# Attention block with multi-query keys on one core: loads of x moved a cycle ahead, two products moved, hand-written orders of the front and the end changed, centred end rows kept in PSUM

## The chip, the cores and the metric

The kernel runs on 1 core of one Trainium2 chip. The metric is the device time of one execution in microseconds (us). Engines are called as in the profile: PE (matmul), PEld (the weight loads of PE, which overlap its matmuls), DVE (vector), ACT (scalar), POOL (GpSimd), SP (the queue that issues nearly all DMAs).

## What is computed

x has 64 sequences of 128 tokens with 512 features. Each gets a pre-normed attention with 16 heads and one shared key and value head of 64, a bias per head, a null key, a causal and a key mask, an output projection, a layer norm, and the residual.

```python
xn = layernorm(x, g_in)
q = (xn @ Wq).reshape(b, n, H, DH).transpose(0, 2, 1, 3) * scale
kv = xn @ Wkv                      # one key and one value head for all 16 query heads
sim = q @ [null_k, k]^T + [null_bias, attn_bias]
sim = where(causal or masked, neg, sim)
out = softmax(sim) @ [null_v, v]
out = layernorm(out @ Wo, g_out)
return x + out
```

## The kernel before, in words

**Tiles and stages.** A group is four sequences. Rows of x come in by `load_x(m)` (L114), one tile of 128 rows by 512 for each m; from the third group on a tile takes a quarter of each of the four sequences, in four DMAs of 64 KB. Such a tile lives in a pool of three buffers (`xp`). `norm_stats(m)` (L282, DVE, then the power -1/2 on POOL), `norm_apply(m)` (ACT, L310) and `tokens_T(m)` (DVE transposes, L331) make it normed and transposed blocks; `tokens_out(g)` (L340) sends a group to DRAM in one DMA and `tokens_in(g)` (L348) reads it back as `xT` in four. `key_values` (L1067; matmuls L358, eviction L373) makes keys and values, `values_send`, `keys_send` and `values_fetch` (L387, L393, L399) move them.

**Products by Strassen.** The query product of a group is seven products of half size instead of eight. `q_one(c, k, h)` (L973) is product k: matmuls in L597, into bank "a" or "c" or a bank of `ps_w`, then an eviction: ACT copies into kept tiles `kp`, `ku` (L608) or into `qT` (L614), DVE sums into `qT` (L617). Products 6, 7 and 4 go on adding onto bank "a" after the copy of the product before; product 3 adds onto bank "c" after DVE's sum of product 7. From cycle 2 (`LEAF`) products 2, 3 and 4 are split once more: `leaf` (L536), matmuls L553, DVE sums L556. The output projection of a pair does the same: `out_one(p, k)` (L1017), matmuls L860, with sums of its inputs on POOL (`out_sum`, L843).

**Scores and softmax.** `region(c)` (L1050) computes the scores of the next two sequences (L651) and the values of the two whose softmax is done (L770). DVE adds scores to mask and bias (L687; the sum `bias_add`, L635, is POOL's), takes maxima (L692); ACT takes exponentials (L701); POOL scales (L722); DVE transposes (`blocks_T`, L737); ACT or DVE evicts the values into `oT` (L810, L808).

**The order of the work** is written out by hand, since the schedule is manual: each engine does its instructions in the order of the program text, and waits only for data and buffers. SP takes DMAs in that order too, so a DMA that waits for its buffer holds up all DMAs behind it. There are three lists: the front (L1289 to L1446) with `q_half` (L429: four matmuls of 256 columns, each in two passes) for the first group, products of the second group, and the first scores; `cycle(c)` (L1071) for c = 1 to 29, one pair of sequences each; and the end (L1451 to L1597) for the last pairs. Even cycles end in `tokens_out` and `tokens_in` of a group (L1258, L1268).

**Padding.** `nc.tensor.addr_align(256, offset=n)` puts the next PE instruction at slot n of a block of 256 by empty instructions ahead of it.

**The end.** `y_half` (L873) gives the last six output rows tiles in SBUF (`y_end`). `stats_part` and `pair_stats` (L902, L909 to L913), `pair_pow` (L917, POOL), `pair_center` (L940: subtract the mean, times g_out, which `gain_copy` has put into PSUM) and `pair_scale` (L946: times 1/sqrt, plus the residual `res`) finish them, `store` (L960) writes them out. `load_res` (L132) loads the residual rows.

Of the kernel before, what the change touches and what calls it, by code (L numbers as in the profile page):

```python
# [17 lines left out]
def kernel(  # L18
# [59 lines left out]
    nc = tc.nc  # L78
# [855 lines left out]
    gain = [gob]  # L934

# [4 lines left out]
    def pair_center(b):  # L940
        mv, rstd = yn[b]
        nc.vector.scalar_tensor_tensor(
            ys[b], ys[b], mv[:, 0:1], gain[0], ALU.subtract, ALU.mult
        )

    def pair_scale(b):  # L946
        mv, rstd = yn.pop(b)
        nc.vector.scalar_tensor_tensor(  # L948
            ys[b], ys[b], rstd, res.pop(b), ALU.mult, ALU.add
        )  # L950
# [4 lines left out]
    def pair_residual(b):  # L955
        nc.vector.tensor_tensor(ys[b], yn.pop(b), res.pop(b), ALU.add)
# [114 lines left out]
    def cycle(c):  # L1071
# [22 lines left out]
        if m < B:  # L1094
            load_x(m)
        if fin:
            pair_pow(r)
# [83 lines left out]
        if fin:  # L1181
            pair_gain(r)
            pair_residual(r)
            store(r)
# [121 lines left out]
    q_half(0, 0)  # L1306
    weights_q(0, 1)
    norm_stats(4)
    weights_kv()
    weights_q(1, 1)  # L1310
    norm_stats(5)
    q_half(1, 0)
    weights_q(2, 1)
    norm_T(2)
    weights_q(3, 1)
    weight_sum(1)
    norm_T(3)
    norm_nmr(4)
    norm_apply(4)
    mask_neg(0)  # L1320
    q_half(2, 0)
    kv_out(0, kv_mm(0))
    kv_out(2, kv_mm(2))
    values_send(0)
    norm_nmr(5)
    null_columns()
    norm_stats(6)
    weight_sum(2)
    q_half(3, 0)
    weight_sum(4)  # L1330
    q_half(4, 0)
    norm_apply(5)
    norm_stats(7)
    norm_nmr(6)
    norm_T(4)
    q_half(5, 0)
    keys_send(0)
    null_shift(0, R8)
    bias_add(0)
    q_half(6, 0)  # L1340
    norm_nmr(7)
    norm_apply(6)
    norm_T(5)
    load_x(10)
    bias_add(1)
    q_half(4, 1)
    load_x(11)
    key_values(4)
    norm_apply(7)
    q_half(7, 0)  # L1350
    values_fetch(0)
    load_null_value()
    norm_T(6)
    norm_T(7)
    token_sum(1, 3)
    region(-1)
    exps(0, 0, 0, 4)
    q_half(5, 1)
    exps(0, 0, 4)
    exps(0, 1, 0, 2)  # L1360
    rinv(0, 0)
    q_half(6, 1)
    scores_max(1, 0)
    token_sum(1, 1)
    token_sum(1, 2)
    scale(0, 0)
    token_sum(1, 4)
    q_half(7, 1)
    q_one(0, 1, 0)
    weight_sum(3)  # L1370
    scores_max(1, 1)
    q_one(0, 2, 0)
    load_x(9)
    load_late()
    exps(0, 1, 2, 4)
    q_one(0, 6, 0)
    load_x(8)
    norm_stats(8)
    exps(1, 0, 0, 4)
    exps(0, 1, 4, 7)  # L1380
    exps(0, 1, 7)
    norm_stats(9)
    norm_stats(10)
# [4 lines left out]
    q_half(1, 1)  # L1388
    q_one(0, 5, 0)
    q_one(0, 7, 0)  # L1390
    norm_stats(11)
    norm_apply(8)
    exps(1, 0, 4)
    rinv(1, 0)
    q_half(0, 1)
    scale(1, 0)
    nc.tensor.addr_align(256, offset=31)
    q_one(0, 4, 0)
    exps(1, 1, 0, 4)
    exps(1, 1, 4)  # L1400
    blocks_T(0)
    bias_add(2)
    rinv(1, 1)
    q_one(0, 3, 0)
    scale(1, 1)
    nc.tensor.addr_align(256, offset=73)
    q_one(0, 1, 1)
    q_one(0, 2, 1)
    out_weight_sum(0)
# [3 lines left out]
    leaf_weights(2, 1)  # L1413
    tokens_T(8)
    key_values(6)
    tokens_T(9)
    leaf_weights(2, 2)
    q_one(0, 6, 1)
    nc.tensor.addr_align(256, offset=138)
    q_one(0, 5, 1)  # L1420
    q_one(0, 7, 1)
    out_weight_sum(1)
    values_send(1)
    norm_apply(10)
    norm_apply(11)
    nc.tensor.addr_align(256, offset=179)
    q_half(2, 1)
    blocks_T(1)
    bias_add(3)
    out_weight_sum(2)  # L1430
    leaf_weights(4, 1)
    q_half(3, 1)
    q_one(0, 4, 1)
    out_weight_sum(3)
    tokens_T(10)
    tokens_T(11)
    leaf_weights(3, 1)
    leaf_weights(3, 2)
    leaf_weights(3, 4)
    q_one(0, 3, 1)  # L1440
    keys_send(1)
    leaf_weights(4, 2)
    leaf_weights(4, 4)
    leaf_weights(2, 4)
    tokens_out(2)
# [8 lines left out]
    load_res(B - 2)  # L1454
# [4 lines left out]
    scores_upper(B - 2, ps_w, "ww")  # L1459
    scores_max(B - 3, 0)  # L1460
    exps(B - 4, 0, 0, 8)
    load_res(B - 4)
# [4 lines left out]
    load_res(B - 3)  # L1467
# [6 lines left out]
    rinv(B - 4, 1)  # L1474
    scores_add(B - 2, 0)
    scores_max(B - 2, 0)
    exps(B - 3, 0, 0, 8)
    scale(B - 4, 0)
# [10 lines left out]
    rinv(B - 3, 0)  # L1489
    load_res(B - 5)  # L1490
    scale(B - 3, 0)
# [7 lines left out]
    pair_pow(B - 8)  # L1499
# [4 lines left out]
    blocks_T(B - 3)  # L1504
    out_one(B - 6, 7, True)
# [12 lines left out]
    out_one(B - 4, 1)  # L1518
    pair_stats(B - 7)
    scores_max(B - 1, 1)  # L1520
# [39 lines left out]
    pair_center(B - 6)  # L1560
    out_one(B - 2, 2)
    out_sum(B - 2, 0)
# [12 lines left out]
    out_sum(B - 2, 2)  # L1575
    pair_center(B - 4)
    out_one(B - 2, 5)
# [4 lines left out]
    stats_part(B - 2, 0)  # L1582
    stats_part(B - 2, 1)
    pair_stats(B - 2)
# [7 lines left out]
    pair_stats(B - 1)  # L1592
    pair_pow(B - 1)
    store(B - 2)
# [40 lines left out]
```

## Time and profile before

| what | value |
|---|---|
| median of three runs | 1035.18 us (1034.01 to 1036.33) |
| the profiled execution, its own time | 1035.38 us |
| its span, first to last instruction | 1033.6 us |
| mean granted clock of PE | 0.997 |
| DMA | 100.90 MB, mean 98 GB/s |

In the page of the profile each engine has its busy time, its share of the span and its count of instructions. Rows of a timeline read: start in us, duration in us, engine, line, operation, output <- input, shape, count, and in brackets the idle time of that engine just before and what ended it. A group of several instructions has one row with their count; a matmul's duration reaches to its modelled end, so the starts say more than the ends. Rows of waits read: engine and line, what it waited for, total us, number of times, the longest. "issue" is a wait for nothing that the profile shows; SPq rows are the issue of DMAs.

### The profile page before, as it was taken

To read this page: it belongs to the slowest core of one execution; us is meant where nothing else is said; L and a number is where in the kernel's file an instruction comes from. 1 tells how busy PE (TensorE), PEld (TensorE's weight loads), DVE (VectorE), ACT (ScalarE), POOL (GpSimd) and SP (SyncE) were. 2 spreads that over 40 slices of the span, in tenths; PEclk is the share of its full clock that TensorE was granted. 3 is DMA by queue.
4 is the path that set the end of the run, shared out by engine and by line. 5 is a ranking of instruction groups with operands and counts; after the bars stand their busy time and mean duration, and the time that the engine had idled before them with its cause. 6 is when DMAs were issued, how large, how long until landed. Compare 5 with 4: busy or idle time off the path is not lost. (4 is left out here: it accounts for less than half of the span.)

```text
span 1033.6 us, 31778 instructions
## 1 busy us (share of the span) xinstructions
PE 1017.9 (98%) x12104; PEld 894.1 (87%) x12104; DVE 864.3 (84%) x2000; ACT 644.0 (62%) x2742; POOL 787.5 (76%) x710
## 2 busy tenths in 40 slices
PE   9999999999999999999999999999999999999996
PEld 8878888889888888888889888888888898888875
DVE  7766888888888898888888888888888988878898
ACT  2655776556775656766557765557756567755581
POOL 3699959588696877959679595886968779596774
PEclk9999999999999999999999999999999999999998
DMA  6541160522506144151521605225051431502202
GB/s 210 164 131 48 73 156 23 149 82 88 151 33 151 59 126 114 72 131 39 147 93 72 167 21 147 75 94 145 32 155 55 129 111 72 126 13 63 83 2 102
DMA packets 70263, 100.90 MB, mean 98 GB/s; under 512 B 27744, under 2 KB 31328, under 8 KB 68320
## 3 DMA queue, kind: packets, MB, share of 16 engines
q1 hardware_dynamic: 69008, 97.83, 33.3%
q8 instruction: 96, 1.57, 0.7%
q10 hardware_dynamic: 1104, 1.05, 0.3%
q14 instruction: 55, 0.45, 0.1%
HBM read 63.19 MB, written 33.55 MB: 94 GB/s over the span
## 5 line engine op out<-in xcount | busy, mean ns | idle before, releaser
L701 ACT ACTIVATE s<-s,nmax 128x65 f32<-128x65 f32 (+1 forms) x1024 | 377.0, 400 | 3.4 <-DVE nmax L692 3.4
L722 POOL TENSOR_TENSOR s<-s,rinv 128x1024 f32<-128x1024 f32 (+1 forms) x128 | 188.5, 1483 | 57.1 <-DVE rinv L718 56.6
L701 ACT ACTIVATION_READ_ACCUMULATOR s<-s,nmax 128x1 f32 x1024 | 229.2, 224 | 0.0
L635 POOL TENSOR_TENSOR s<-biasp,mneg 128x1552 f32<-128x1552 f32 x64 | 205.0, 3225 | 2.3 <-DMA x<-in_x_dram 2.0
L810 ACT ACTIVATE oT<-poX,nv 128x256 f32<-128x256 f32 x58 | 27.6, 476 | 219.8 <-PE poX L770 112.7
L556 DVE TENSOR_TENSOR qT<-pl,qT 128x128 f32<-128x128 f32 (+1 forms) x420 | 128.6, 329 | 9.5 <-PE pl L553 6.9
L687 DVE TENSOR_TENSOR s<-ps,s 128x256 f32<-128x256 f32 (+2 forms) x224 | 120.1, 604 | 15.7 <-PE ps L651 15.2
L860 PE MATMUL pyX<-wo,oT 128*128 128x256 f32 x512 | 121.5, 380 | 0.0
L692 DVE TENSOR_REDUCE nmax<-s 128x8 f32<-128x520 f32 (+1 forms) x128 | 118.8, 949 | 0.1
L860 PE MATMUL pyX<-wT,oT 128*128 128x256 f32 x488 | 115.5, 380 | 0.8 <-POOL oT L843 0.8
L737 DVE STREAM_TRANSPOSE sb<-s 128x1536 f32<-128x1536 f32 x64 | 112.9, 1764 | 0.2 <-POOL s L722 0.2
L860 PEld LDWEIGHTS pyX<-wo,oT 128*128 128x128 f32 x512 | 96.9, 190 | 14.6 <-issue 0.9
L860 PEld LDWEIGHTS pyX<-wT,oT 128*128 128x128 f32 x488 | 88.4, 190 | 10.8 <-POOL oT L843 1.2
L651 PE MATMUL ps<-kT,qT 64*64 64x128 f32 (+1 forms) x4096 | 93.6, 245 | 1.0 <-issue 1.0
L917 POOL TENSOR_TENSOR rstdo<-rstdo,nhalf 128x1 f32<-128x1 f32 x64 | 35.5, 557 | 75.6 <-PE pl L553 68.3
L651 PEld LDWEIGHTS ps<-kT,qT 64*64 64x64 f32 x4096 | 85.5, 134 | 6.0 <-issue 2.6
L289 POOL TENSOR_TENSOR rstd<-rstd,nhalf 128x1 f32<-128x1 f32 x64 | 37.3, 583 | 65.2 <-DVE rstd L288 59.2
L770 PE MATMUL pos<-sb,vr 32*64 32x128 f32 (+1 forms) x1792 | 81.8, 321 | 0.0
L770 PE MATMUL poY<-sb,vr 32*64 32x128 f32 x720 | 74.8, 347 | 0.2 <-issue 0.2
L770 PE MATMUL poX<-sb,vr 32*64 32x128 f32 x960 | 73.7, 299 | 0.0
L503 ACT COPY qT<-pa 128x256 f32<-128x256 f32 x168 | 66.7, 397 | 1.4 <-PE pa L597 1.4
L860 PE MATMUL pyw<-wo,oT 128*128 128x256 f32 x280 | 66.4, 380 | 0.3 <-POOL oT L843 0.2
(150 smaller groups left out, 2514.8 us busy)
## 6 DMA issues: line engine op xcount, KB each, us to landing
res<-in_x_dram SPq DMA_DIRECT2D x64, 256.0 KB, 3.0
out_dram<-y SPq DMA_DIRECT2D x58, 256.0 KB, 2.0
x<-in_x_dram SPq DMA_DIRECT2D x224, 64.0 KB, 2.7
xd<-xb SPq DMA_DIRECT2D x14, 1024.0 KB, 3.9
xT<-xd SPq DMA_DIRECT2D x56, 256.0 KB, 5.9
vr<-vd SPq DMA_DIRECT2D x64, 128.0 KB, 2.7
x<-in_x_dram SPq DMA_DIRECT2D x8, 256.0 KB, 4.9
vd<-vt SPq DMA_DIRECT2D x32, 64.0 KB, 2.2
```

What stands on the lines that cost most here:

```text
L289: nc.gpsimd.tensor_tensor(rstd, rstd, nhalf, ALU.pow)
L503: nc.scalar.copy(q_part(g, c, h), by_block("a"))
L556: nc.vector.tensor_tensor(o, p, o, ALU.add)
L635: nc.gpsimd.tensor_tensor(S[b], biasp, mneg[:, t].unsqueeze(1).broadcast_to([P, R8, ROW]), ALU.add,)
L651: nc.tensor.matmul(to[r][i * DH : (i + 1) * DH, f, :], qT[g, f // FH, t // GH][rows, f % FH, t % GH, NQ - 1 - i if hf else i], kT[g][rows, ...
L687: nc.vector.tensor_tensor(sv, ps, sv, ALU.add)
L692: nc.vector.tensor_reduce(nmax[b][:, hf], S[b][:, :, WITH_NULL[hf]], AX.X, ALU.max, negate=True)
L701: nc.scalar.activation(row, row, AF.Exp, bias=nmax[b][:, hf, k : k + 1], accum_out=rsum[b][:, hf, k : k + 1],)
L722: nc.gpsimd.tensor_tensor(sv, sv, rinvs.pop((b, hf)).unsqueeze(2).broadcast_to([P, R8, sv.shape[2]]), ALU.mult,)
L737: nc.vector.transpose(sb.rearrange("p j e q -> p e j q"), S[b][:, :, 1 : ROW - 1].rearrange("p e (j k) -> p e j k", k=Q),)
L770: nc.tensor.matmul(po[s][rows, half], vr[g][quad(s), j, t, :], sb[quad(s), slots, r * NF : (r + 1) * NF, :], start=start, stop=True, skip_ ...
L860: nc.tensor.matmul(prod[key], h[:, c, :], w[:, c, :], start=(start and c == 0), stop=(c == HC - 1), skip_group_check=not start,)
```

## The change

1. **Loads of x.** `load_x(m)` and `load_x(m + 1)`, which each cycle issued for its own use, go. Each cycle now issues `load_x(m + 2)` ahead of `store(r)` and `load_x(m + 3)` ahead of `tokens_out`, for the next cycle; cycle 1 issues its own two at its start as well.
2. **Two products of cycle 1** (the only pass of `cycle` with c < LEAF): product 4 goes behind `out_one(p, 2)`, product 3 goes ahead of product 1 of the other half.
3. **The front.** The list after `q_half(0, 0)` is in a new order, for all engines; the offsets of the paddings are 40, 97, 146 and 211 in place of 31, 73, 138 and 179.
4. **The end.** Some steps of its list trade places.
5. **Centred rows.** For the last six rows `pair_center` writes into a PSUM tile (two rows a tile, tag "s"), and `pair_scale` reads that and writes `ys`.

```diff
     def pair_center(b):
         mv, rstd = yn[b]
+        if b < B - 6:
+            o = ys[b]
+        else:
+            if b // 2 not in yns:
+                yns[b // 2] = ps_s.tile([P, 2, DIM], FP, tag="s", name=f"yc_{b}")
+            o = y_mid[b] = yns[b // 2][:, b % 2]
         nc.vector.scalar_tensor_tensor(
-            ys[b], ys[b], mv[:, 0:1], gain[0], ALU.subtract, ALU.mult
+            o, ys[b], mv[:, 0:1], gain[0], ALU.subtract, ALU.mult
         )
...
-            ys[b], ys[b], rstd, res.pop(b), ALU.mult, ALU.add
+            ys[b], y_mid.pop(b, ys[b]), rstd, res.pop(b), ALU.mult, ALU.add
...
-        if m < B:
+        if c == 1:
             load_x(m)
+            load_x(m + 1)
...
         q_one(c, 7, 0)
-        if m + 1 < B:
-            load_x(m + 1)
...
         if c >= LEAF:
             q_one(c, 8, 0)
-        else:
+        out_one(p, 2)
+        if c < LEAF:
             q_one(c, 4, 0)
-        out_one(p, 2)
...
             exps(b0, 1, 0, 6)
+        if c < LEAF:
+            q_one(c, 3, 0)
         q_one(c, 1, 1)
...
-        if c < LEAF:
-            q_one(c, 3, 0)
...
             pair_residual(r)
+        if m + 2 < B:
+            load_x(m + 2)
+        if fin:
             store(r)
...
             q_one(c, 4, 1)
+        if m + 3 < B:
+            load_x(m + 3)
         if first and toks:
             tokens_out(m // GB)
```

The new front, PE's steps in their order with the padding, and of the others the steps that the text below names (`...` where steps are left out):

```python
q_half(0, 0); weights_kv(); weights_q(2, 1); q_half(1, 0); norm_T(2); weights_q(3, 1); norm_T(3); load_x(11)
...
q_half(2, 0); kv_out(0, kv_mm(0)); kv_out(2, kv_mm(2)); weight_sum(1); weight_sum(2); values_send(0)
q_half(3, 0); keys_send(0); q_half(4, 1); q_half(4, 0); null_shift(0, R8); bias_add(0); bias_add(1)
q_half(5, 0); norm_T(4); norm_T(5); q_half(7, 0); key_values(4); norm_T(6); q_half(6, 0); load_x(10); norm_T(7)
region(-1); token_sum(1, 3); scores_max(1, 0); weight_sum(4)
q_half(5, 1); load_late(); rinv(0, 0); load_x(9); q_half(6, 1); q_one(0, 1, 0); q_half(7, 1); weight_sum(3)
q_one(0, 2, 0); q_one(0, 5, 0); q_one(0, 6, 0); load_x(8); values_fetch(0); q_half(1, 1); q_one(0, 7, 0)
q_half(0, 1); q_one(0, 4, 0); addr_align(256, offset=40)
q_one(0, 3, 0); key_values(6); norm_apply(10); q_one(0, 1, 1); addr_align(256, offset=97)
q_one(0, 2, 1); q_half(2, 1); blocks_T(1); out_weight_sum(0); bias_add(3); addr_align(256, offset=146)
q_one(0, 6, 1); values_send(1); keys_send(1); q_one(0, 5, 1); q_one(0, 7, 1); q_half(3, 1); addr_align(256, offset=211)
q_one(0, 4, 1); tokens_T(11); tokens_out(2); q_one(0, 3, 1); region(0)
```

The old one from the same place, PE's steps:

```python
q_half(5, 1); q_half(6, 1); q_half(7, 1); q_one(0, 1, 0); q_one(0, 2, 0); q_one(0, 6, 0); q_half(1, 1); q_one(0, 5, 0)
q_one(0, 7, 0); q_half(0, 1); addr_align(256, offset=31); q_one(0, 4, 0); q_one(0, 3, 0); addr_align(256, offset=73)
q_one(0, 1, 1); q_one(0, 2, 1); key_values(6); q_one(0, 6, 1); addr_align(256, offset=138); q_one(0, 5, 1); q_one(0, 7, 1)
addr_align(256, offset=179); q_half(2, 1); q_half(3, 1); q_one(0, 4, 1); q_one(0, 3, 1); region(0)
```

The end, the parts that matter:

```diff
-    out_one(B - 6, 2)
+    out_one(B - 6, 5)
+    out_one(B - 6, 2)
+    scores_add(B - 1, 0)
     scores_upper(B - 1, ps_s, "s")
-    out_one(B - 6, 5)
...
     pair_center(B - 5)
     out_sum(B - 2, 1)
     out_sum(B - 2, 3)
+    pair_scale(B - 5)
     pair_pow(B - 3)
-    pair_center(B - 3)
     pair_scale(B - 6)
     store(B - 6)
-    pair_scale(B - 3)
-    store(B - 3)
-    pair_scale(B - 5)
+    out_one(B - 2, 5)
     store(B - 5)
     pair_pow(B - 4)
+    pair_center(B - 3)
+    pair_scale(B - 3)
     out_sum(B - 2, 2)
     pair_center(B - 4)
-    out_one(B - 2, 5)
+    stats_part(B - 2, 0)
     pair_scale(B - 4)
```

Beside these, residual loads are issued in another order at the start of the end's list, and `pair_pow(B - 8)`, `pair_stats(B - 7)`, `scale`, `store(B - 3)` and `store(B - 2)` move by a few places.

More of the change, by code (lines that the diff above doesn't have):

```diff
@@ L1323 @@
     kv_out(2, kv_mm(2))
+    weight_sum(1)
+    norm_apply(5)
+    weight_sum(2)
     values_send(0)
-    norm_nmr(5)
+    q_half(3, 0)
+    norm_stats(6)
+    norm_nmr(6)
+    keys_send(0)
     null_columns()
-    norm_stats(6)
-    weight_sum(2)
-    q_half(3, 0)
-    weight_sum(4)
[L1331 to L1357, printed above, removed]
-    q_half(5, 1)
[L1359 to L1363, printed above, removed]
+    q_half(4, 1)
+    norm_stats(7)
+    q_half(4, 0)
+    null_shift(0, R8)
+    norm_nmr(7)
+    bias_add(0)
+    bias_add(1)
@@ L1364 @@
+    q_half(5, 0)
+    norm_apply(6)
+    norm_T(4)
+    norm_T(5)
+    q_half(7, 0)
+    norm_apply(7)
+    key_values(4)
+    norm_T(6)
+    q_half(6, 0)
+    load_x(10)
+    norm_T(7)
+    region(-1)
+    token_sum(1, 3)
+    exps(0, 0, 0, 4)
+    scores_max(1, 0)
+    weight_sum(4)
+    q_half(5, 1)
     token_sum(1, 1)
     token_sum(1, 2)
+    load_late()
+    exps(0, 0, 4)
+    rinv(0, 0)
+    exps(0, 1, 0, 2)
+    load_x(9)
+    q_half(6, 1)
+    scores_max(1, 1)
     scale(0, 0)
     token_sum(1, 4)
+    q_one(0, 1, 0)
```

109 lines of the change are left out of this document (55 added, 54 removed).

## The prediction

> **What bounds the kernel now.** I read the shares of the engines first, then the starts of the scores along PE's timeline, then the waits, at last the few windows where PE stands still.
>
> ```profile
> PE 1017.9 (98%) x12104; PEld 894.1 (87%) x12104; DVE 864.3 (84%) x2000; ACT 644.0 (62%) x2742; POOL 787.5 (76%) x710
> ```
>
> PE is the bound nearly everywhere, and the change takes no matmul away. So it can win only where PE stands, and after PE's last matmul. How much PE stands in the cycles is read from the starts of the score matmuls, one row for each cycle:
>
> ```profile
> 128.45 2.91 PE L651 MATMUL ps<-kT,qT 64*64 64x128 f32 x128
> ...
> 566.30 2.91 PE L651 MATMUL ps<-kT,qT 64*64 64x128 f32 x128
> 597.34 2.91 PE L651 MATMUL ps<-kT,qT 64*64 64x128 f32 x128
> 628.44 2.91 PE L651 MATMUL ps<-kT,qT 64*64 64x128 f32 x128
> 661.03 2.91 PE L651 MATMUL ps<-kT,qT 64*64 64x128 f32 x128
> ...
> 941.21 2.91 PE L651 MATMUL ps<-kT,qT 64*64 64x128 f32 x128
> ```
>
> An odd cycle can take 31.04 us (566.30 to 597.34), an even one 31.10 (597.34 to 628.44), yet the odd one from 628.44 takes 32.59. From the first row to the last are 13 odd and 13 even cycles in 812.76 us; at 62.14 a pair they would take 807.8. So **4.9 us** are lost there, 1.55 of them in the one cycle. Who is late:
>
> ```profile
> PEld pl L553 <- DVE qT L556: 6.4, 14, 1.0
> ```
> ```profile
> DVE st L284 <- DMA x<-in_x_dram: 8.0, 9, 2.0
> ```
> ```profile
> 630.91 4.34 SPq L348 DMA_DIRECT2D xT<-xd  x4
> 636.94 7.11 SPq L128 DMA_DIRECT2D x<-in_x_dram  x8
> ```
> ```profile
> 644.30 0.69 DVE L284 BATCH_NORM_STATS2 st<-x 128x6 f32<-128x512 f32 x1 [1.98 <-DMA x<-in_x_dram]
> ```
> ```profile
> 645.98 0.49 PE L553 MATMUL pl<-xL,wq 128*128 128x128 f32 x2 [0.59 <-DVE qT L556]
> ```
>
> Between 110 and 960 us PE's weight loads wait 14 times for the sums of the small products (6.4 us), and in the cycles between 180 and 960 us DVE waits 9 times for a tile of x (8.0 us). The rows of the bad cycle join the two: SP issues x behind the four reads of xT, eight issues take 7.11 us, the statistics of x stand 1.98 us for the tile, the sum behind them comes that late, and PE stands for the sum.
>
> **Part 1, loads a cycle ahead.** A tile then has a whole cycle of some 31 us in hand, where the first is now issued 7.4 us before its use (636.94 to 644.30), so DVE's 8.0 us of waits go. Not all of that was PE's loss: the upper bound is the 4.9 us above, a lower one the 1.55 of this cycle alone. I take **-4.4**, near the upper end, since the sums are the only wait besides steady ones in this stretch, and leave 0.5 for what may belong to others. What is late next in an undisturbed cycle is nothing on PE: 31.04 is reached now.
>
> What the moved loads pass on SP: in an odd cycle `load_x(m + 2)` stands behind the reads of the values and ahead of a store which is not ready for some time anyway; in an even cycle `load_x(m + 3)` comes ahead of the send of the tokens:
>
> ```profile
> 618.94 0.70 DVE L331 STREAM_TRANSPOSE xb<-x 128x512 f32<-128x512 f32 x1
> ```
> ```profile
> 623.70 0.33 SPq L340 DMA_DIRECT2D xd<-xb  x1
> 629.49 1.25 SPq L387 DMA_DIRECT2D vd<-vt  x2
> ```
> ```profile
> 642.63 1.89 PE L358 MATMUL pkv<-xT,wkv 128*128 128x256 f32 x8
> ```
>
> Its buffer is free once the transpose at 618.94 is done, at 619.64. Four issues at the slowest rate seen above (7.11 / 8 = 0.89 us) end at 623.2, ahead of 623.70. So the send isn't late: cost nothing, covered by the time in which SP waits for the second transpose.
>
> **Parts 2 and 3, cycle 1 and the front.** PE's standing there:
>
> ```profile
> 50.62 1.03 PE L597 MATMUL pc<-xT,wS 128*128 128x256 f32 x4
> 51.99 1.13 PE L597 MATMUL pa<-xT,wq 128*128 128x256 f32 x4 [0.35 <-ACT qT L614]
> ...
> 55.55 1.03 PE L597 MATMUL pa<-xS,wS 128*128 128x256 f32 x4
> 57.16 1.10 PE L597 MATMUL pc<-xS,wS 128*128 128x256 f32 x4 [0.58 <-DVE kT L373]
> ```
> ```profile
> 74.94 1.03 PE L597 MATMUL pa<-xS,wq 128*128 128x256 f32 x4
> 76.58 1.13 PE L597 MATMUL pa<-xS,wq 128*128 128x256 f32 x4 [0.61 <-ACT ku L608]
> 77.55 1.89 PE L860 MATMUL pyw<-wo,oT 128*128 128x256 f32 x8
> 79.28 1.03 PE L597 MATMUL pa<-xT,wq 128*128 128x256 f32 x4
> ```
>
> Eight matmuls of 256 columns take 1.73 us (77.55 to 79.28), a product of four 0.87. So the first two gaps are 51.99 - 50.62 - 0.87 = 0.50 and 57.16 - 55.55 - 0.87 = 0.74; PE's next start behind such a gap is 0.1 late again (76.58 to 77.55 is 0.97). Front: 1.4 us can be won; cycle 1: 76.58 - 74.94 - 0.87 + 0.1 = 0.87.
>
> I followed the new front by hand with the durations of the trace, each engine in its new order. Up to the first scores PE finds everything in time; tightest is `key_values(4)`, ready 0.1 us ahead. Behind them, product (0, 3, 0) comes right when DVE's sum of product 7 is done, since `weight_sum(4)`, a further 1.2 us, now stands ahead of it; and (0, 6, 1) comes some 0.3 before ACT's copy, which has `norm_apply(10)` ahead of it. Padding by offsets less matmul slots (four each) is 25 empty instructions in three places as before, one more in the first: taken as nothing, as these run ahead of PE's queue. Of 1.4 us some 0.3 come back: **-1.1**, with bounds of -1.4 and +1.4 (the same waits kept and as much again).
>
> In cycle 1 product 4 behind `out_one(p, 2)` has its copy in time. But ACT now evicts product 4 about 0.9 later, so its exponentials are later by that, while PE runs 0.9 earlier; ACT has idle 1.1 us before the copies later in the cycle, so about 0.6 of the gain is lost before product 3 of the second half. And the reads of xT for group 2 start behind four more loads:
>
> ```profile
> 68.46 2.28 SPq L348 DMA_DIRECT2D xT<-xd  x4
> ```
>
> They move from 68.46 to about 70; 4.34 us is the longest issue of such four above, and the key product that needs them would start at 79 instead of 81. That is in time, but barely. I take **-0.2** (bounds: -0.87 and +1.5).
>
> **Part 4, the list of the end.** Product 5 ahead of product 2 covers a wait for a bank, but the next stop is POOL's sum, whose chain starts at the same matmul as before:
>
> ```profile
> 988.92 1.99 PE L860 MATMUL pyw<-wo,oT 128*128 128x256 f32 x8 [0.19 <-POOL oT L843]
> ```
>
> PE starts again at 988.92 either way: **0**. Bounds: 0.5 either way, PE's standing there.
>
> **Part 5, the tail.** PE's last matmuls start at 1023.72, but DVE still has work:
>
> ```profile
> 1017.30 1.39 DVE L942 SCALAR_TENSOR_TENSOR y_end<-y_end,mvo,gain 128x512 f32<-128x512 f32 x2
> 1018.61 0.90 DVE L948 SCALAR_TENSOR_TENSOR y_end<-y_end,rstdo,res 128x512 f32<-128x512 f32 x1
> 1019.96 2.42 DVE L948 SCALAR_TENSOR_TENSOR y_end<-y_end,rstdo,res 128x512 f32<-128x512 f32 x2 [0.44 <-POOL rstdo L917]
> ...
> 1027.59 0.41 DVE L885 TENSOR_TENSOR y_end<-pyw,kyu 128x256 f32<-128x256 f32 x1
> ...
> 1029.84 0.75 DVE L948 SCALAR_TENSOR_TENSOR y_end<-y_end,rstdo,res 128x512 f32<-128x512 f32 x1
> ```
> ```profile
> 1023.72 1.89 PE L860 MATMUL pyw<-wT,oT 128*128 128x256 f32 x8
> ```
> ```profile
> L942 DVE SCALAR_TENSOR_TENSOR y_end<-y_end,mvo,gain 128x512 f32<-128x512 f32 x6 | 4.3, 737 | 0.0
> L948 DVE SCALAR_TENSOR_TENSOR y_end<-y_end,rstdo,res 128x512 f32<-128x512 f32 x6 | 5.6, 943 | 0.7 <-POOL rstdo L917 0.4
> L953 DVE TENSOR_TENSOR yn<-yn,gob 128x512 f32<-128x512 f32 x56 | 38.9, 694 | 10.3 <-ACT yn L932 10.3
> ```
>
> The six with both inputs in SBUF take 943 ns, 0.90 to 1.21 while POOL sums and 0.75 alone; the six with `gain` in PSUM hold 737 beside the same sums. With one input in PSUM the scales should hold some 0.74: 5.6 - 6 x 0.74 = 1.2 saved. The 0.44 for POOL's power goes too, as two scales now stand ahead of the one that needs it: 1.6. The trace has no such scale writing from PSUM; L953 reads and writes PSUM in 694 ns, so its bounds are 0.69 and 0.94, the gain 0.4 to 1.9. [...]
>
> Does PE then decide? Its last result is there at 1023.72 + 1.73 = 1025.5 and some latency, and DVE takes it at 1027.59, 2.1 later. A gain of 1.6 leaves DVE behind PE still. I take **-1.4**, as a scale waits some 0.1 for the step ahead of it in either form.
>
> **Sum**, against the profiled execution's own 1035.38: -4.4 - 1.1 - 0.2 + 0 - 1.4 = -7.1, which gives **1028.3 us**. That execution stands 0.2 above the median shown.
>
> **Rivals.**
> - *Front and cycle 1 give all back* (a new wait for each one removed, ACT and DVE being full there): 1035.4 - 4.4 - 1.4 = 1029.6; with their upper bounds, 1032.5. For it: two margins of 0.1 us and none above 0.5. Against: PE's gaps there are three and each has new work in it. Chance 0.23.
> - *The loads don't pay*: DVE's wait was only what showed first, and the sums are late for another cause in the same cycles (the reads of xT, say); then part 1 gives 0 to -1: 1035.4 - 0.5 - 2.7 = 1032.2. Against: nothing else is late at 644.30. Chance 0.10.
> - *No net change*: parts 1 and 5 as in the rival above, and the front loses 2: about 1035. Chance 0.08.
> - *Slower: the loads hold up the tokens.* SP is in order, so where the four loads of an even cycle issue slower, the send of 623.70 goes late.
>
> ```profile
> xd<-xb SPq DMA_DIRECT2D x14, 1024.0 KB, 3.9
> xT<-xd SPq DMA_DIRECT2D x56, 256.0 KB, 5.9
> ```
>
> The send has 630.91 - 623.70 - 3.9 = 3.3 us before the reads of xT notice, and these land by 630.91 + 4.34 + 5.9 = 641.2, 1.5 ahead of the key product. From 619.64 the loads would have to take over 4.1 + 4.8 = 8.9 us, 2.2 an issue. Beyond that 14 even cycles pay each: at 2.4 an issue 14 x 0.7 = 10 us, which gives 1028.3 + 10 = 1038. Against: 0.89 is the slowest mean seen. Chance 0.12.
>
> **Chances.** The forecast's case has 0.47, with 1026.5 to 1029.5 of its own. Faster by over 0.2% (2.1 us, about what a measurement of this kernel tells from no change): 0.47 + 0.23 + 0.08 of the second = 0.78; within 0.2%: 0.02 + 0.08 = 0.10; slower: 0.12. The range is 1025.5 to 1035.5: its low end is the sum of the best bounds (-4.9 - 1.4 - 0.9 - 0.5 - 1.9 = -9.6), the high end takes in the first three rivals.
>
> **What will show it.** Part 1: no row of DVE waiting for x in the cycles, and all odd cycles near 31.04, so 941.21 - 128.45 falls to about 808.3. Parts 2 and 3: the first scores of `region(0)`, now at 64.36, start near 63.2, with no wait of PE for ACT's copies. Part 4: the product at 988.92 still waits for POOL. Part 5: scales near 0.74, and from PE's last matmul to the end of the span 1.4 us less. The prediction is wrong if xT comes late in cycle 1 or in odd cycles (key products waiting for a DMA), or if PE meets waits for its instructions in new places.

## The result, and the profile after

The changed kernel takes **1027.64 us** (median of four runs, 1027.56 to 1027.81); the kernel before took 1034.6 beside it (1033.1 to 1036.33). The ratio is 0.9932, with a 95% interval of 0.9915 to 0.9950: faster by 0.7%. The profiled execution has 1027.59 us and a span of 1025.8 at a clock of 0.999; the span before was 1033.6.

From the page of the changed kernel, its row of engine shares:

```profile
PE 1013.1 (99%) x12104; PEld 895.4 (87%) x12104; DVE 863.5 (84%) x2000; ACT 643.9 (63%) x2742; POOL 785.7 (77%) x710
```

DVE and ACT are as busy as before. From its timeline, the scores that open the regions -1, 0 and 1, those of cycle 3, of three cycles in the middle and of cycle 29:

```profile
33.89 2.91 PE L651 MATMUL ps<-kT,qT 64*64 64x128 f32 x128
63.73 2.91 PE L651 MATMUL ps<-kT,qT 64*64 64x128 f32 x128
95.53 2.91 PE L651 MATMUL ps<-kT,qT 64*64 64x128 f32 x128
127.25 2.91 PE L651 MATMUL ps<-kT,qT 64*64 64x128 f32 x128
...
593.18 2.91 PE L651 MATMUL ps<-kT,qT 64*64 64x128 f32 x128
624.27 2.91 PE L651 MATMUL ps<-kT,qT 64*64 64x128 f32 x128
655.30 2.91 PE L651 MATMUL ps<-kT,qT 64*64 64x128 f32 x128
...
934.90 2.91 PE L651 MATMUL ps<-kT,qT 64*64 64x128 f32 x128
```

The cycle that took 32.59 takes 655.30 - 624.27 = 31.03; from cycle 3 to cycle 29 it is 934.90 - 127.25 = 807.65 us, 5.1 less. What waits for x there is gone. Rows of waits between 110 and 960 us, first PE's weight loads and then DVE (what waits, for what: total, times, longest):

```profile
PEld pa L597 <- issue: 10.4, 27, 0.4
PEld poX L770 <- issue: 4.6, 27, 0.2
PEld pa L597 <- ACT qT L503: 4.4, 15, 0.7
PEld pa L597 <- POOL rstdo L917: 4.3, 13, 0.3
PEld pl L553 <- DVE qT L1008: 0.3, 1, 0.3
```
```profile
DVE rinv L718 <- ACT s L701: 36.1, 57, 1.1
DVE y L885 <- PE pyY L860: 31.2, 27, 1.3
DVE qT L1008 <- ACT qT L503: 11.7, 39, 0.3
```

PE's 14 waits for the small sums (6.4 us) and DVE's waits for x (8.0 us) have no row any more; what is left is the steady part of each cycle.

The starts of the scores cut every kernel into stages. This table is the main tool of the study: each column is a difference of two such starts in one profiled execution, "end" runs from the scores of the last region to the end of the span.

| kernel | to first scores | front | cycle 1 | cycle 2 | 3 to 28 | cycle 29 | end |
|---|---|---|---|---|---|---|---|
| before | 33.86 | 30.50 | 32.34 | 31.75 | 812.76 | 30.06 | 62.33 |
| changed | 33.89 | 29.84 | 31.79 | 31.73 | 807.65 | 30.04 | 60.85 |
| loads alone | 33.59 | 30.53 | 32.33 | 31.77 | 807.76 | 30.05 | 62.46 |
| changed, old front | 33.61 | 30.58 | 31.80 | 31.72 | 807.67 | 30.04 | 60.59 |
| changed, old cycle 1 | 33.93 | 29.84 | 32.33 | 31.73 | 807.68 | 30.05 | 60.94 |
| changed, centred rows in SBUF | 34.01 | 29.84 | 31.79 | 31.73 | 807.76 | 30.05 | 61.71 |
| changed, old end, SBUF | 33.68 | 29.78 | 32.27 | 31.75 | 807.76 | 30.06 | 62.51 |
| changed, padding ahead of q_half | 33.49 | 29.52 | 31.80 | 31.75 | 807.76 | 30.06 | 61.52 |
| changed again | 33.55 | 29.82 | 32.27 | 31.73 | 807.76 | 30.05 | 60.80 |
| changed, padding ahead of the wait | 34.37 | 28.94 | 31.80 | 31.77 | 807.76 | 30.05 | 61.31 |
| changed, order of cycle 1 | 35.62 | 29.84 | 31.51 | 32.03 | 807.76 | 30.06 | 61.49 |
| changed, padding and reads | 33.94 | 28.94 | 31.79 | 31.73 | 807.76 | 30.06 | 61.08 |

The 7.8 us of span are 5.1 in the cycles, 0.66 in the front, 0.55 in cycle 1 and 1.48 in the end. The first column lies anywhere from 33.49 to 35.62, and the last from 60.59 to 61.52 for the eight kernels that have the changed end, so a small edit is read from its own stage and not from the whole time.

### The profile page after: what moved, and what is told of

Same layout as the page of the kernel before. It is cut to its first block, busy times and chain, and to the rows that moved or that the text cites. A ratio compares the mean times of both kernels' runs of the same rounds, so it can differ in the third digit from the quotient of the medians.

```text
span 1025.8 us, 31861 instructions
## 1 busy us (share of the span) xinstructions
PE 1013.1 (99%) x12104; PEld 895.4 (87%) x12104; DVE 863.5 (84%) x2000; ACT 643.9 (63%) x2742; POOL 785.7 (77%) x710
## 3 DMA queue, kind: packets, MB, share of 16 engines
q8 instruction: 96, 1.57, 0.7%
HBM read 63.19 MB, written 33.55 MB: 94 GB/s over the span
## 5 line engine op out<-in xcount | busy, mean ns | idle before, releaser
L701 ACT ACTIVATION_READ_ACCUMULATOR s<-s,nmax 128x1 f32 x1024 | 231.7, 226 | 0.0
L917 POOL TENSOR_TENSOR rstdo<-rstdo,nhalf 128x1 f32<-128x1 f32 x64 | 35.0, 548 | 80.4 <-PE pl L553 74.2
```

Source lines behind the costliest of these rows:

```text
L701: nc.scalar.activation(row, row, AF.Exp, bias=nmax[b][:, hf, k : k + 1], accum_out=rsum[b][:, hf, k : k + 1],)
```

## The experiments

The theory: each part of the change works in its own stage, by the waits that the forecast named. The rivals: the loads pay only together with the front, or the order of SP's queue is itself the harm; the end was won by its list and not by PSUM.

**Loads alone** (the kernel before with part 1).

```diff
-        if m < B:
-            load_x(m)
+        if c == 1:
+            load_x(m)
+            load_x(m + 1)
...
+        if m + 2 < B:
+            load_x(m + 2)
         if fin:
             store(r)
...
+        if m + 3 < B:
+            load_x(m + 3)
```

> The kernel before with part 1 alone (loads of x a cycle ahead). Theory (x came late behind the reads of xT, its lateness went through DVE's statistics and sums to PE): the stretch from the scores of cycle 3 to those of cycle 29 falls from 812.8 to about 807.6 us, all odd cycles at 31.03 to 31.04; front and end stay as before; so about 1030 us (1029.7 to 1030.5), and its runs lie within a few tenths of each other instead of 3 us. Rival (the loads pay only together with the new front or the moved products, or the sums are late for another cause in the same cycles): 1033 to 1035, with odd cycles still up to 1.5 us too long.

Measured: 1030.31 us (1029.7 to 1031.19) against 1034.58, ratio 0.9963 (0.9951 to 0.9976). Its row of the table has the whole gain of cycles 3 to 28 and nothing else. The rival is out: the loads pay by themselves, 5.0 us in the profile. Its runs spread over 1.5 us, less than the 3.7 of before beside it, but not the few tenths that were expected.

**Four places for the loads** (the changed kernel, the place of the next odd cycle's loads changing with the even cycle).

```diff
+        own = c % 2 and c > 1 and (c // 2) % 4 == 3
+        late = (c // 2) % 4 if first else 0
...
+        if late == 2 and m + 2 < B:
+            load_x(m + 2)
+        if late in (1, 2) and m + 3 < B:
+            load_x(m + 3)
```

> The changed kernel with the loads for the next odd cycle at four places in turn, by even cycle: as changed; the second tile behind the four reads of xT; both tiles behind them; both in the odd cycle itself at the old places. One kernel, read by the length of each odd cycle. Theory (what counts is whether the tile has landed when DVE comes to its statistics about 16 us into the cycle): the first three all take 31.03, since loads right behind the reads land some 3 us ahead; only the fourth is longer, by 0.1 to 1.5. Rival (to stand behind the reads is the harm itself): second and third are longer too, in this order.

Measured: 1027.83 us (one execution). Behind the reads of xT, one tile or both: 31.03 in all of these cycles (3, 5, 11, 13, 19, 21). So to stand behind the reads is no harm in itself. Loaded in the odd cycle itself: 31.03, 31.12 and 31.15 (cycles 7, 15, 23). In the second of these DVE waited, from the timeline of this run:

```profile
514.29 0.69 DVE L284 BATCH_NORM_STATS2 st<-x 128x6 f32<-128x512 f32 x1 [0.51 <-DMA x<-in_x_dram]
```

and in the kernel before, three of its ten such rows:

```profile
142.84 0.70 DVE L284 BATCH_NORM_STATS2 st<-x 128x6 f32<-128x512 f32 x1 [0.51 <-DMA x<-in_x_dram]
...
205.83 0.69 DVE L284 BATCH_NORM_STATS2 st<-x 128x6 f32<-128x512 f32 x1 [1.01 <-DMA x<-in_x_dram]
...
518.46 0.69 DVE L284 BATCH_NORM_STATS2 st<-x 128x6 f32<-128x512 f32 x1 [1.40 <-DMA x<-in_x_dram]
```

Set beside the excess of the cycle over 31.04, all ten waits of before give one rule:

| DVE's wait, us | 0.23 | 0.36 | 0.40 | 0.51 | 0.61 | 0.96 | 1.01 | 1.04 | 1.40 | 1.98 |
|---|---|---|---|---|---|---|---|---|---|---|
| the cycle's excess, us | 0 | 0 | 0 | 0.08 | 0.18 | 0.54 | 0.58 | 0.62 | 0.97 | 1.55 |

PE loses what DVE waits beyond 0.43 us, to within 0.02. The run with four places fits it: 0.51 gave 0.09, and a wait of 0.54 in cycle 23 gave 0.12; cycle 7 had no wait and lost nothing. One even cycle of that run (24) took 31.27; the next experiment comes back to it.

**The send held up** (the changed kernel, the tile ahead of the send loaded 0 to 3 times over).

```diff
+        if first and m + 3 < B:
+            for _ in range(c // 2 % 4):
+                for i in range(GB):
+                    nc.sync.dma_start(
+                        out=xs[m + 3][quad(i)],
+                        in_=x[(m + 3) // GB * GB + i, 3 * Q : 4 * Q, :],
+                    )
         if first and toks:
             tokens_out(m // GB)
```

> The changed kernel with the second tile of an even cycle loaded again 0, 1, 2 or 3 times over, in turn by cycle, ahead of the send of the tokens; each repeat waits for the one before to land and so holds SP up for some 3.5 to 4 us more. It adds 64 KB x 4 a repeat and changes no result. It measures from which lateness of the send a cycle gets longer: the forecast's rival of a slower kernel had 4.8 us of room (3.3 until the reads of xT notice, 1.5 more until the key product of the next odd cycle). Theory: one repeat is free, two cost 0 to 2 us in the next odd cycle, three cost 3 to 6 us. If the room is smaller than worked out, one repeat costs already; if it is larger, two and three are free.

Measured: 1031.48 us (one execution), but not by the curve that was expected. The send stands 4.74 us ahead of the odd cycle's scores in the changed kernel; here, by repeats (times from the starts of the scores; the fetch is the start of the first 16 KB packet of the instruction queue q8 around these scores, from the trace's DMA records):

| repeats | odd cycles | send, to the scores | fetch, to the scores | cycle, us |
|---|---|---|---|---|
| 0 | 9, 17, 25, 27 | -4.71, -4.72, -4.59, -4.74 | -0.52, -0.55, -0.35, -0.42 | 31.06, 31.04, 31.04, 31.04 |
| 1 | 3, 11, 19 | -3.82, -4.47, -4.27 | -0.13, -0.34, -0.41 | 31.04, 31.04, 31.05 |
| 2 | 5, 13, 21 | -2.36, -2.46, -2.18 | +1.77, +1.72, +1.93 | 32.32, 32.15, 32.39 |
| 3 | 7, 15, 23 | -0.29, +1.13, -0.34 | -0.36, -0.52, -0.36 | 31.04, 31.39, 31.04 |

With three repeats the send is 4.4 us late twice at no cost, and 5.9 us late once for 0.36 (PE's key product waits 0.3 there). So the room lies between 4.4 and 5.9 us; the forecast had worked out 4.8. The cost at two repeats, 1.1 to 1.35, is another thing, with PE standing inside the region. From the timelines of SP and PE in cycle 13:

```profile
436.35 0.42 SPq L340 DMA_DIRECT2D xd<-xb  x1
...
441.99 1.99 SPq L348 DMA_DIRECT2D xT<-xd  x4
```
```profile
442.83 0.32 PE L770 MATMUL pos<-sb,vr 32*64 32x128 f32 x2 [0.72 <-issue]
```

PE waits there for nothing that the profile shows. The DMA view of 440.4 to 441.6 us has a packet of instructions:

```profile
q8 instruction: 1, 0.02, 4.8%
```

Where the send goes out 2.2 to 2.5 us ahead of the scores, the fetch, elsewhere 0.1 to 0.6 ahead of them, begins only 4.1 to 4.2 us behind the send, at +1.7 to +1.9. Where the send goes out later still, the fetch has begun before it. That the fetch queues behind the 1 MB of the send is read from these times, the same in all three cycles of a kind; no run moved the fetch by itself, so it is likely and not shown.

A late fetch also goes with the even cycles that took too long. In cycles 4 and 12 of the kernel before (31.36 and 31.29 us) and in cycle 24 of the run with four places (31.27) it begins 0.80, 0.73 and 0.79 us behind the scores, and PE loses 0.26, 0.19 and 0.18 inside the region. In all other cycles from 3 to 28 of the fourteen profiles, those with two repeats apart, it begins at +0.44 or earlier, and no such cycle is longer by more than 0.04 us, but for what DVE's waits or the late send account for. In the six cycles with a late fetch PE goes on 1.4 to 1.6 us after the packet's end. The even cycles have no send, so what made the fetch late there is open. All three follow an odd cycle that loads x at the old place: there are 16 such even cycles in the profiles, and none of the 166 others has it.

**The old front** (the changed kernel; the list from `q_half(0, 0)` to `region(0)` and its offsets as before, as the change's diff shows them).

> The changed kernel with the old front: order and offsets of the kernel before from q_half(0, 0) to region(0), all else as changed. Theory (the front gave 0.66 us, from two waits less and one new standing of 0.83): the stretch from the scores of the first to those of the second region goes from 29.84 back to 30.50, so 1028.2 to 1028.4, unless cycle 1 takes part of it back. Rival (the front's order also carries part of what cycle 1 shows, since ACT and DVE enter it in another order): 1028.7 or more, with cycle 1 longer than 31.79 too.

Measured: 1028.75 us (1027.84 to 1029.95), ratio 0.9950 (0.9938 to 0.9963). The front goes back to 30.58, cycle 1 stays at 31.80: theory. The median is 0.4 above what the stage gives, within the scatter of its runs.

**The padding.** The rows that the changed kernel's front rests on, of PE and then of its sequencer:

```profile
49.79 1.03 PE L597 MATMUL pa<-xS,wq 128*128 128x256 f32 x4
51.48 0.45 PE L597 MATMUL pc<-xT,wS 128*128 128x256 f32 x1 [0.67 <-issue]
```
```profile
L1414 PEldq NOP  x30: 13/13/13, 49.1 to 51.4; - x30
```

Product 4 ends its issue at 49.79 + 0.87 = 50.66 and product 3 starts at 51.48: PE stands 0.82. The 30 empty instructions of `addr_align(256, offset=40)` take 2.3 us, and end right there. In the kernel before the same 30 ran 45.9 to 48.2, well ahead. Here they begin only at 49.1, since the sequencer, in order, has stood until 49.0 for ACT's copy which product 4 waits for, and that copy ended at 48.59 + 0.37 = 48.96:

```profile
48.59 0.37 ACT L608 COPY ku<-pa 128x256 f32<-128x256 f32 x1
```

The kernel before had the same standing in another place. Its third padding, of 25, begins when product 6 has ACT's copy (54.95 + 0.36 = 55.31) and ends where product 5 starts:

```profile
L1419 PEldq NOP  x25: 13/13/13, 55.4 to 57.1; - x25
```
```profile
55.20 0.37 DVE L617 TENSOR_TENSOR qT<-pc,ku 128x256 f32<-128x256 f32 x1
```

PE had work until 55.55 + 0.87 = 56.42, and product 5 started at 57.16. The row in the prediction puts this gap down to DVE's eviction of the keys (L373). But product 5 neither reads the keys nor writes their bank, and the last reader of its own bank, the sum of DVE above, was done at 55.57. So the 0.74 us that the forecast counted as a wait for DVE were the padding's own. This is read from the rows; no run moved that padding alone.

For the padding of the changed kernel two places were tried.

```diff
     leaf_weights(2, 1)
+    nc.tensor.addr_align(256, offset=16)
     q_half(0, 1)
     q_one(0, 4, 0)
...
-    nc.tensor.addr_align(256, offset=40)
     q_one(0, 3, 0)
```

> The changed kernel with the first padding of the front put ahead of q_half(0, 1), at offset 16 instead of 40, so that every matmul keeps its place in the block of 256 and the same 30 empty instructions stand 24 places earlier. Theory (PE stands 0.83 us ahead of product (0, 3, 0) since the 30 empty instructions, 71 ns each, stand right behind a wait of the sequencer for ACT's copy): the empty instructions are done before that wait, the standing goes, the scores of region(0) start 0.6 to 0.8 earlier, about 1026.9 us. Rival (product (0, 3, 0) in truth waits for DVE's sum of product 7, as the forecast had it): PE stands at the same place as long, 1027.6.

Measured: 1027.66 us (1027.08 to 1027.83). Neither: the front gains 0.32 of 0.83. The empty instructions (31 by the trace, not 30) now end at 48.1 and PE stands ahead of `q_half(0, 1)`:

```profile
L1407 PEldq NOP  x31: 13/13/13, 45.7 to 48.1; - x31
```
```profile
46.80 1.03 PE L597 MATMUL pa<-xS,wq 128*128 128x256 f32 x4
48.16 1.97 PE L437 MATMUL pq<-xT,wq 128*128 128x256 f32 x8 [0.34 <-issue]
```

PE has work until 46.80 + 0.87 = 47.67, so the lead at 45.7 was 1.97 us, for 2.4 of padding. In the changed kernel it was 50.66 - 49.1 = 1.56. The next place lies 16 instructions on, still ahead of the wait:

```diff
     q_half(0, 1)
+    nc.tensor.addr_align(256, offset=32)
     q_one(0, 4, 0)
```

> The changed kernel with the first padding between q_half(0, 1) and q_one(0, 4, 0), at offset 32: the same 30 empty instructions, now ahead of the sequencer's wait for ACT's copy and not right behind it, and behind the earlier wait by 16 instructions more than in the run with the padding ahead of q_half(0, 1), where PE still stood 0.58. Theory (the cost is the lead that the sequencer has over PE when it comes to the padding): PE stands nowhere from the scores of the first region to those of the second but for the steady restarts, that stretch falls from 29.84 to about 29.0, and the time by 0.6 to 0.8 against the changed kernel beside it, less what the wait for instructions in the end's list takes back (it was 0.83 in the changed kernel's profile, 0.56 to 1.5 in others). Rival (these 2.1 us of empty instructions cost 0.6 to 0.8 wherever they stand): 29.5 or more.

```profile
L1408 PEldq NOP  x31: 13/13/13, 46.6 to 49.0; - x31
```
```profile
47.68 1.03 PE L597 MATMUL pa<-xS,wq 128*128 128x256 f32 x4
48.54 1.89 PE L437 MATMUL pq<-xT,wq 128*128 128x256 f32 x8
50.27 1.03 PE L597 MATMUL pa<-xS,wq 128*128 128x256 f32 x4
51.13 1.03 PE L597 MATMUL pc<-xT,wS 128*128 128x256 f32 x4
```

The front takes 28.94: the theory. The padding ends 1.3 us ahead of product 4 (50.27), and nothing stands. The time, 1027.72 (1027.06 to 1028.75), is 0.4 below that of the changed kernel beside it, 1028.12 (1027.68 to 1028.63). The profiled execution began its first scores 0.8 later and lost 0.5 in the end, so the whole time does not settle it; the stage does.

**Old products in cycle 1** (the changed kernel; product 4 ahead of `out_one(p, 2)`, product 3 behind `leaf(c, 2, 1)` again).

> The changed kernel with the two products of cycle 1 at their old places. Theory (product 4 stood 0.78 us for ACT's copy, and half of the gain is lost again ahead of product 3 of the second half): the stretch from the scores of region(0) to the next goes from 31.79 back to about 32.3, 1028.1 to 1028.3. Rival (cycle 1 gained by the loads or the front, and not by the products): 31.8 stays, 1027.6.

Measured: 1028.34 us (1027.93 to 1028.73), cycle 1 at 32.33. Theory: 0.54 is the products' own. The sequencer stood 1.47 us for the reads of xT in this profile, but PE has no gap ahead of the key product, so the reads have no part in it.

**The changed kernel again.**

> The changed kernel once more, unaltered, on the chip of the next two runs: what they are measured against. 1027.6 as at first, if the reads of xT in cycle 1 are always just in time; up to 0.7 more in some executions if not.

Measured: 1028.12 us, and in its profiled execution cycle 1 took 32.27. So it did in the run with the old end, which shares this code. PE's sequencer on the key product's line, in this run and then in the changed kernel's first profile (shortest, median, longest wait):

```profile
L358 PEldq EVENT_SEMAPHORE  x2: 51/866/1682, 78.0 to 78.1; - x2
```
```profile
L358 PEldq EVENT_SEMAPHORE  x2: 51/51/51, 78.4 to 78.5; - x2
```

The sequencer stood 1.68 us for the reads of xT, which the two loads of cycle 1 had pushed back, and PE stood 0.74 ahead of the key product. The cycle is longer by 0.48 only, since PE, later by then, no longer waits 0.4 ahead of product 3 of the second half.

**Order of cycle 1** (the changed kernel).

```diff
         if c == 1:
             load_x(m)
-            load_x(m + 1)
...
             tokens_in(2)
+            load_x(m + 1)
...
-        if toks:
+        if toks and c >= LEAF:
             norm_apply(m + 1)
...
+        if toks and c < LEAF:
+            norm_apply(m + 1)
```

> The changed kernel with two steps of cycle 1 moved: the reads of xT go between its two loads of x (as before the change), and norm_apply(m + 1) goes behind q_one(c, 7, 1), so that ACT's copy of product 7 no longer stands behind it. Theory: the wait of 0.40 ahead of product 3 of the second half goes, cycle 1 takes about 31.4 instead of 31.79, and the key product has the reads 1.5 us earlier, so the executions in which it waited (0.74 in the profile of the run with the old end) are gone: 0.4 less than the changed kernel beside it, and a spread of a few tenths. Rival (DVE's transposes behind the moved norm come late and PE waits there instead): 31.8 or more.

Measured: 1028.24 us (1027.82 to 1030.09). The wait ahead of product 3 is gone and cycle 1 takes 31.51, but cycle 2 takes 32.03 in place of 31.73: moving `norm_apply` won 0.28 and gave 0.30 back. The 0.30 stand ahead of one small product of cycle 2, which starts 0.41 us late for a sum of DVE where it was 0.10 late: the rival in kind, one cycle later. The path from the moved norm to that sum was not traced.

**Centred rows in SBUF** (the changed kernel; `pair_center` writes `ys[b]` for all rows).

> The changed kernel with the centred rows of the end back in SBUF, in the new order of the end. Theory (a scale with both inputs in SBUF is slowed while POOL sums): in the new order about half of the six scales lie beside POOL's work, those take 0.9 to 1.2 instead of 0.75, so 0.4 to 0.7 longer than the changed kernel's 1027.6: 1028.0 to 1028.3. If all six are slowed as the forecast's term had it: 1.2 longer, 1028.8. Rival (the new order of the end won it all): no change, 1027.6, and the scales near 0.75 though they read SBUF.

Measured: 1028.87 us (1028.68 to 1029.34). The end is 0.86 longer. Its scales, from DVE's timeline, with POOL's work beside them:

```profile
1011.46 2.09 DVE L950 SCALAR_TENSOR_TENSOR y_end<-y_end,rstdo,res 128x512 f32<-128x512 f32 x2
...
1014.30 1.44 DVE L950 SCALAR_TENSOR_TENSOR y_end<-y_end,rstdo,res 128x512 f32<-128x512 f32 x1
...
1016.66 0.73 DVE L950 SCALAR_TENSOR_TENSOR y_end<-y_end,rstdo,res 128x512 f32<-128x512 f32 x1
```
```profile
1011.07 1.27 POOL L843 TENSOR_TENSOR oT<-oT 128x512 f32<-128x512 f32 x1
...
1013.93 1.27 POOL L843 TENSOR_TENSOR oT<-oT 128x512 f32<-128x512 f32 x1
```

and the six scales of the changed kernel as one group:

```profile
L955 DVE SCALAR_TENSOR_TENSOR y_end<-yc,rstdo,res 128x512 f32<-128x512 f32 x6 | 4.4, 746 | 0.3
```

It is not that all six are slower. The pair from 1011.46 takes 2.09 for 1.41 in the changed kernel, the one from 1014.30 takes 1.44 for 0.75, and the others take 0.73 to 0.75. So two of six are longer, by 0.68 and 0.69, and both are issued while a sum of POOL runs. At 1.43 and 1.44 us they are longer than the 0.9 to 1.2 of the theory. The second ends at 1015.74, and POOL's sum at 1015.20 (its spans are rough), 0.54 before. The same holds in two more kernels with the rows in SBUF: the longer scales take 0.90 and 1.75 in the kernel before, 0.92 and 1.76 with the old end, 1.43 and 1.44 here, and each ends 0.54 or 0.55 us behind the end of a sum of POOL. By these ends they wait for that sum, they are not merely slowed. With one input in PSUM nothing like it shows: in the changed kernel two scales begin beside POOL's sum of 1011.05 to 1012.31 and one beside that of 1013.31 to 1014.58, and they take 0.74 to 0.75 like the other three. Why DVE waits for POOL when both inputs are in SBUF was not shown. POOL's work is longer there too: its power (L917) takes 0.55 us as a rule, but 1.01 in the kernel before where it begins at 1018.92 beside the scale of 0.90 (1.00 beside the long scales of the other two), and that power is the one that DVE then stood 0.44 for.

**The old end, rows in SBUF** (the changed kernel with the old list of the end, and `pair_center` writing `ys[b]`).

> The changed kernel with the old list of the end and the centred rows in SBUF (parts 4 and 5 undone). Theory: the stretch from the scores of the last cycle to the end goes back from 60.85 to about 62.3 us, so 1029.1. What it is longer than the run with the centred rows in SBUF alone is the share of the new order: by the forecast about 0.4 (the wait for POOL's power), at most 1. Rival (the 1.5 us of the end came with the other parts, through PE's restarts at the start of the list): under 0.7 longer, 1028.3 or less.

Measured: 1029.42 us (1028.43 to 1029.85). The end is 62.51, as before the change, and 62.51 - 61.71 = 0.80 longer than with the rows in SBUF alone. Two rows cut the end into three parts: a group of score matmuls early in the list, and the last sum of the pair before the last. Here is first the one and then the other, each for the kernel before, the changed one, the one with rows in SBUF and this one:

```profile
978.57 1.50 PE L651 MATMUL ps<-kT,qT 64*64 64x64 f32 x58 [0.95 <-issue]
```
```profile
971.93 1.50 PE L651 MATMUL ps<-kT,qT 64*64 64x64 f32 x58 [0.40 <-issue]
```
```profile
971.95 1.50 PE L651 MATMUL ps<-kT,qT 64*64 64x64 f32 x58 [0.40 <-issue]
```
```profile
972.66 1.50 PE L651 MATMUL ps<-kT,qT 64*64 64x64 f32 x58 [0.40 <-issue]
```
```profile
1012.21 0.41 DVE L885 TENSOR_TENSOR y_end<-pyw,kyu 128x256 f32<-128x256 f32 x1
```
```profile
1005.57 0.41 DVE L885 TENSOR_TENSOR y_end<-pyw,kyu 128x256 f32<-128x256 f32 x1
```
```profile
1005.60 0.41 DVE L885 TENSOR_TENSOR y_end<-pyw,kyu 128x256 f32<-128x256 f32 x1
```
```profile
1006.40 0.41 DVE L885 TENSOR_TENSOR y_end<-pyw,kyu 128x256 f32<-128x256 f32 x1
```

| kernel | from the scores of the last region to the first row, us | on to the second row | on to the end of the span |
|---|---|---|---|
| before | 7.30 | 33.64 | 21.39 |
| changed | 6.98 | 33.64 | 20.23 |
| changed, centred rows in SBUF | 6.76 | 33.65 | 21.30 |
| changed, old end, SBUF | 7.37 | 33.74 | 21.40 |

In the tail PSUM won 1.07 of 1.16 and the order 0.09. In the middle part, where the list has product 5 ahead of product 2, nothing is won. The first part has the same matmuls in every kernel, and PE's only waits there are for nothing that the profile shows, as where a packet of instructions came late: with the new list it takes 6.76 to 7.68 us in the profiles, with the old one 7.30 to 7.41. So 0.61 of the 0.80 lie within this scatter, and the list's own share is at most 0.2. The same scatter took back what the padding's first place had won in the front (7.68 there).

**Padding and reads together** (the changed kernel; padding ahead of the wait, and the reads of xT between the two loads).

```diff
             tokens_in(2)
+            load_x(m + 1)
...
     q_half(0, 1)
+    nc.tensor.addr_align(256, offset=32)
     q_one(0, 4, 0)
```

> The changed kernel with the first padding ahead of the wait (as in the run that took the front's stretch to 28.94) and with the reads of xT of cycle 1 between its two loads of x again; norm_apply stays where the change has it, since cycle 2 gave back what cycle 1 won by it. Theory: front stretch 28.9 to 29.0, cycle 1 always 31.8 and never 32.3, so the two stretches together 60.7 to 60.8 instead of 61.6 (or 62.1 when the reads came late); the time 0.9 below the changed kernel where its reads were just in time, 1027.0 or a little above, as the start of the program and the wait for instructions in the end scatter by as much. Rival (the loads behind the reads come late for DVE's statistics in cycle 1): cycle 1 at 32 or more.

Measured: **1027.16 us** (1026.80 to 1028.95) against 1033.94, ratio 0.9937 (0.9924 to 0.9951). Front 28.94, cycle 1 31.79 in its profile. The lowest median and the lowest single run of the study, but over the whole time it can't be told from the changed kernel (0.9939, 0.9927 to 0.9952, in its second measurement).

## Why the prediction was right, point by point

- **Loads** (forecast -4.4, bounds -1.55 to -4.9): -5.1, and -5.0 alone. Mechanism right, size too small by 0.7. The mechanism of the forecast, DVE's wait for x in the odd cycles, is worth 4.52 (the sum of the table's excesses), close to the 4.4. The even cycles that had lost 0.26 and 0.19 came back too, and there the fetch of instructions was late (0.80 and 0.73 us behind the scores), which the forecast did not see. That the wait of PE follows from DVE's wait for x was argued from one cycle; the table of ten waits shows it.
- **The send is not held up** (nothing): right. 623.70 - 597.34 = 26.36 before; 619.53 - 593.18 = 26.35 after, by this row of SP:

```profile
619.53 0.34 SPq L340 DMA_DIRECT2D xd<-xb  x1
```

- **Front** (-1.1): -0.66. The step that failed is "taken as nothing, as these run ahead of PE's queue". The empty instructions cost 0.82, as a wait stands just ahead of them. The trace of the kernel before had it already: of the two gaps that the forecast read as waits for ACT and DVE, the second was padding (0.74). Of the two waits that the forecast put in their place, product (0, 3, 0) for DVE's sum and (0, 6, 1) for ACT's copy, neither is there once the padding is moved: the front is then 30.50 - 28.94 = 1.56 shorter than before, more than the bound of 1.4.
- **Cycle 1** (-0.2): -0.55 where the reads of xT were in time, -0.07 where they were not. Both parts of the working hold: ahead of product 3 of the second half 0.4 comes back (0.6 forecast), and the reads are "in time, but barely". The forecast took one value for what is two cases, and missed both. The key product that waits for a DMA was among its signs of being wrong; it came in two profiles, at 0.48 us.
- **The list of the end** (0): right, and for the reason given. PE still stops for POOL's sum, and that stretch takes 33.64 us in both kernels.
- **Tail** (-1.4): -1.16. The scales take 746 ns (0.74 forecast). But the "0.90 to 1.21 while POOL sums" was a misreading: the row of 2.42 us holds one scale of 0.75 and one of 1.75, so only two of six were long in the kernel before too, for the wait and not by a rate. The 0.44 for POOL's power, which the forecast gave to the order, goes with the same wait, the other way round. By the runs the order is worth 0.09: it removes DVE's wait for the power, but with rows in SBUF its two long scales together then take 1.37 us more than 0.75 each, where those of the old order took 1.15 more.
- **Sum**: -7.8 of span against -7.1 (by the medians the gain is 7.0, as the profiled execution of the kernel before was 0.8 above its median). The loads gave 0.7 more, cycle 1 0.35 more, and the front 0.44 less. That the end's 1.48 meets the 1.4 is in part luck: the tail gave 1.16, and 0.32 came from less standing at the start of the list in that one profile. The low end of the range was given as 1025.5; 1035.38 - 9.6 is 1025.8. The case of the forecast is the one that came; that the front and cycle 1 would give all back, or the loads not pay, is out. The slower rival (the send late by over 4.8 us) has about the room that it was given, but in the changed kernel the send is not late at all.

## What to carry to other kernels

Follow a late DMA to the engine that bounds: the loss is the wait less the slack between them, here 0.43 us by ten waits of different length. An order written by hand is also an order of PE's sequencer: put padding ahead of a wait, at a place where the sequencer's lead over PE is longer than the padding. Behind the wait, with a lead of 1.56 us, 2.3 us of it cost 0.82 here; ahead of the wait, with a lead of 3.6, 2.4 us cost nothing. Cut the span into stages by a matmul that every cycle has, and judge an edit of half a microsecond by its stage.

## What the runs showed of the hardware that was not expected

- Stops of PE that the profile puts down to nothing go with late packets of instructions. The instruction queue q8 has 96 packets of 16 KB (1.57 MB by the page); that PE's instructions come by it is read from these stops. In the three cycles with two repeats a packet that elsewhere began 0.1 to 0.6 us ahead of the scores began 4.1 to 4.2 us behind the send of 1 MB, 1.7 to 1.9 behind the scores, and PE stood 0.7 to 1.0 us. In even cycles, which have no send, three fetches that began 0.73 to 0.80 us behind the scores went with a loss of 0.18 to 0.26. In cycles 3 to 28 of the changed kernel each fetch begins at +0.27 or earlier, and none shows a loss: the odd cycles take 31.03, the even ones 31.09 or 31.10.
- An empty instruction takes some 76 ns of PE's sequencer (30 in 2.3 us). Where the sequencer's lead over PE was 1.56 us, PE stood 0.82; with 1.97 it stood 0.5; with 3.6 (46.6 to the start of product 4 at 50.27) it did not stand. In the kernel before, 25 of them (1.8 us) met a lead of 56.42 - 55.4 = 1.0, and PE stood 0.74.
- A scale of DVE with both inputs in SBUF that begins beside a sum of POOL ends 0.54 or 0.55 us behind that sum, in six of six cases, whether it then takes 0.90 or 1.76 us.
